# Cross-attention block on one core: score units worked off in sixteen pairs, with the maxima chain, the values' product, the reciprocal chain and the scaling done once for each pair

## The chip, the cores and the metric

The kernel runs on 1 core of one Trainium2 chip. A core has TensorE (PE, matrix products into eight PSUM banks of 128 x 512 fp32), VectorE (DVE), ScalarE (ACT), GpSimd (POOL) and SyncE (SP, which here issues all DMAs). PEld is PE's weight load. The metric is device microseconds of one execution; a kernel's time is the median of its runs. Everything is fp32.

## The reference

x and ctx are 8 sequences of 256 tokens by 512 channels. The block has 16 heads of 32 channels and an MLP of width 2048:

```
q = (layer_norm(x, ln1) @ q_w + q_b) ; k, v = ctx @ k_w + k_b , ctx @ v_w + v_b      # split in 16 heads of 32
scores = einsum("bhqd,bhkd->bhqk", q, k) / sqrt(32) ; scores = where(mask, scores, finfo.min)
out = einsum("bhqk,bhkd->bhqd", softmax(scores), v)
hidden = out @ cproj_w + cproj_b + x
y = gelu_tanh(layer_norm(hidden, ln2) @ fc_w + fc_b) @ proj_w + proj_b
return hidden + y
```

## The kernel before, in words

The eight sequences are worked in two groups g = 0, 1 of four. Every large product (q, k, v, the output projection o, and the MLP's fc and pd) is cut as in Strassen's method into seven products P1 to P7 of quarter matrices, summed up in three PSUM banks X, Y and W; the quarters are first added to one another on DVE or POOL, and the results leave PSUM by additions on DVE and copies on ACT.

Nothing is ordered by the hardware or by a scheduler. The kernel first records all operations (`Order.op`), each with the engines it may run on; `Order.run` then replays them in the order of a long list of words, `PROGRAM`. A word is an operation's name, and ":V", ":A" or ":G" behind it chooses DVE, ACT or POOL. A second list, `PLACES`, says which SBUF slot or PSUM bank each buffer takes. So the order on each engine, and what each buffer waits for, stand in these two tables. In tiles that take the same place one after another, the trace shows one of the names.

The attention has 32 units: a group g, four of the 16 heads (hg) and one sequence b. For each:

- `scores` (L1020 on): eight row-tiled matmuls (32 rows, 256 columns, the group "s" on PE) put k times q, keys in the partitions and queries along the row, into four banks. Eight evictions ev (L614, ACT, 128x256) add the mask's bias and write pr.
- the maxima chain: two transposing reductions of 128x1024 (L1033, DVE), three small copies mc that bring the partitions' quarters together (L1039, ACT), a fold of 32x256 to 32x32 (L1040, DVE), a 32x32 transpose (L1042, DVE), a store md to DRAM, and a load mm that broadcasts the maxima to all partitions (512 KB). Each store and load goes through SP's queue.
- less (L1053 on DVE, as one 128x1024, or L1057 on POOL, as two 128x512) subtracts the maxima, exp (L1060, ACT) takes the exponential, for each of two halves.
- in units of kind "z" ss (L625) adds the two key halves of the weights, so that the sums over keys need four ones-matmuls; in units of kind "p" there is no ss, and eight ones-matmuls. `KINDS` holds the kind of each unit: 16 are "z" and 16 are "p".
- `attend`: the column-tiled group av on PE writes the sums (from the ones-matmuls) and the eight values' products into the two halves of one bank. Then the reciprocal chain on DVE, a reduction (L1083), a reciprocal (L1085) and a transpose (L1086), and the scaling att = av * r (L625, 128x256).

PE works in three tilings: full for the large products, row-tiled for s and column-tiled for av. Units of a group come in an order of their own (`units_of`), and PROGRAM spreads them among the products of k, v, q of group 1, of o and of fc.

Of the kernel before, what the change touches and what calls it, by code (L numbers as in the profile page):

```python
# [21 lines left out]
SLOTS = {"Q": (45, 1024), "P": (36, 512), "H": (14, 256), "sm": (10, 32), "mx": (3, 352)}  # L22

BANKS = ("W", "C")
# [12 lines left out]
class Op:  # L37
    __slots__ = (
        "n", "alts", "fn", "deps", "users", "vt", "bufs", "name", "mode", "table", "serve", "base", "start",
        "end", "eng", "stream", "waiting", "ready", "lead", "psum_of", "after", "lock", "pieces",  # L40
# [3 lines left out]
class Order:  # L44
# [9 lines left out]
    def op(self, name, alts, reads, writes, fn, mode="full", table=None, serve=0.0, base=0.0, lead=0.0, lock=False, pieces=1):  # L54
# [5 lines left out]
        o.deps, o.users, o.vt, o.bufs, o.lead = [], [], None, [], lead  # L60
        o.start = o.end = o.eng = None
# [61 lines left out]
cq0_00_0 turn_c0_10_0 turn_c0_00_0 vw00 c0_10_0:A c0_00_0:V small v0_0_P1a cq0_00_1 turn_c0_00_1 c0_00_1:A cq0_01_1  # L123
turn_c0_10_1 v0_0_P1b c0_10_1:V v0_1_P1a cq0_01_0 turn_c0_11 cq0_11_0 c0_11:V vw10 cq0_11_1 kw00 vw11 v0_0_t1:A
turn_c0_01 cq0_10_0 cq0_10_1 c0_01:V c0t1:V v0_1_P1b v0_1_t1:A rows1 vws1:V turn_c0_31 turn_c0_21 vws3:G c0_21:A rows7
vws2:G c0_31:A k0_1_P1 xt0_3 vw01 k0_0_P1 rows3 turn_c0_20 c0t2:V fw0_11_0 v0_0_P6 stats_x0_11 c0t3:V vws4:V rows0
turn_c0_30 fw0_11_1 fw0i4_1:G v0_0_t2:A xt0_2 aggr_x0_11 rows2 v0_1_P6 stats_x0_10 c0_20:A aggr_x0_10 kw10 v0_0_P5
rows5 c0_30:A eps_x0_1 v0_0_P2 rows4 rows6 fw0_10_0 c0t4:V v0_1_t2:V v0_0_t3:A pow_x0_1 nb_x0_1 norm_x0_11:A mk kw11
rows8 v0_1_P2 fw0_00_1 v0_0_P3 kws3:V mk~1 fw0i4_3:G fw0_10_1 cols fw0_00_0 xt0_5 v0_1_P5 fw0i4_2:V xt0_6 fw0i4_4:V
kws1:V kws2:V cols~1 k0_0_t1:A k0_1_t1:V xt0_0 k0_1_P6 v0_0_c11 xt0_7 fw0_01_0 fw0s3:V v0_1_t3:A xt0_1 fw0s1:G  # L130
fw0i5_1:G v0_1_c11 stats_x0_31 k0_0_P7 stats_x0_21 k0_1_t2:A fw0i5_2:G kw01 xt0_4 fw0_01_1 fcd0_5_False fcd0_7_False
stats_x0_00 fw0i5_3:V fw0i1_1:V fcd0_4_True fw0i7_1:G fw0i1_3:V k0_0_P6 qw00 k0_0_t2:A aggr_x0_00 fw0i7_2:V fw0i7_4:V
v0_1_P3 fw1_01_0 k0_1_P2 k0_0_P5 fw0i1_2:V fw0s2:V norm_x0_10:A aggr_x0_21 fw1_00_0 qw11 aggr_x0_31 fw0i5_4:V qw01
fw0i1_4:V k0_1_P5 vd0_0_11 stats_x0_01 aggr_x0_01 fw1_01_1 eps_x0_0 v0_1_c12:A kws4:G fw0i7_3:V v0_0_c12:A stats_x0_20
# [24 lines left out]
k1_0_t1:A c1t2:G k1_1_P6 exp020_1 ev030_31 ev030_20 ev030_11 k1_0_c11 mc010_1 mc010_2 mc010_3 c1t3:G kd0_1_12
ss020_0:V ev030_10 kd0_1_21 mm022 xt1_4 k1_0_P6 k1_0_t2:A ss020_1:V xt1_0 av020 stats_x1_31 mx030_1 mx030_0 aggr_x1_31  # L160
fold010 k1_1_t2:A s012 xt1_6 stats_x1_30 ev012_21 fcd1_7_True mc030_2 mc030_1 ev012_31 xt1_1 r020 k1_1_P5 stats_x1_01
att020 mf010 k1_0_P5 mm002 mc030_3 aggr_x1_30 xd1_2 kd0_0_22 k1_0_P7 less022_1:G exp022_1 md010 less022_0:G
stats_x1_00 ev012_20 exp022_0 ss022_0:V ev012_01 vd0_0_21 ku011 less002_1:V ev012_00 k1_0_t3:A mm010 less002_0:V
ev012_30 ev012_11 ev012_10 aggr_x1_01 k1_1_t3:A fold030 vd0_0_12 ss022_1:G av022 c1t4:G exp002_0 s032 vu010 xt1_5
vu030 ev032_30 ev032_11 mf030 aggr_x1_00 k1_0_c22 mx012_1 vd0_1_11 k1_1_P3 ev032_10 ev032_20 ss002_0:G mx012_0 k1_0_P3
ku001 ev032_01 ev032_31 eps_x1_3 eps_x1_0 ev032_00 less010_1:V exp002_1 k1_1_P7 ss002_1:G k1_0_P4 ev032_21 mx032_1
exp010_1 k1_0_c12:A mx032_0 vd0_0_22 stats_x1_20 av002 mc032_2 md030 mc032_3 ku021 mc032_1 k1_0_c21 r022 fold032
att022 mf032 k1_1_c12:A ku003 pow_x1_0 r002 mc012_1 s001 stats_x1_21 mc012_3 att002 k1_1_P2 less010_0:G ss010_1:G
exp010_0 vu011 nb_x1_0 mm030 k1_1_c22 ss010_0:G ev001_11 aggr_x1_21 ev001_31 vu012 pow_x1_3 ev001_30 md032 vu032 ku031
ev001_00 ev001_01 ev001_21 aggr_x1_20 av010 ev001_10 ev001_20 s021 ku023 k1_1_c11 k1_1_P4 norm_x1_01:A eps_x1_2  # L170
# [336 lines left out]
def tile_xattn_block(  # L507
# [41 lines left out]
    halves = {}  # L549

    def tile_of(b):
        if b.t is None:
# [917 lines left out]
    with tc.manual_schedule():  # L1470
        for o in order:
            o.fn(o.eng)
# [41 lines left out]
```

## Time and profile before

| | |
|---|---|
| median of 3 runs | 655.94 us (653.59 to 657.04) |
| span of the profiled execution | 652.0 us |
| PE busy | 644.3 us |
| DVE busy | 583.2 us |
| POOL busy | 395.9 us |
| ACT busy | 346.1 us |
| granted PE clock, all stages | 1.00 |

The profile is of one execution, and its span is 3.9 us shorter than the median of the runs, so what is worked out from the profile is compared with 652.0 us first. An engine's busy time is the time that its instructions took, not the time that the kernel would save without them: only an idle gap of PE, or work of PE, is surely in the way. A row of groups reads: line, engine, operation, written tile <- read tiles, shape, count, then busy time in all, mean ns of one, and the idle time ahead of them with what ended it.

### The profile page before, as it was taken

To read this page: it belongs to the slowest core of one execution; us is meant where nothing else is said; L and a number is where in the kernel's file an instruction comes from. 1 tells how busy PE (TensorE), PEld (TensorE's weight loads), DVE (VectorE), ACT (ScalarE), POOL (GpSimd) and SP (SyncE) were. 2 spreads that over 40 slices of the span, in tenths; PEclk is the share of its full clock that TensorE was granted. 3 is DMA by queue.
4 is the path that set the end of the run, shared out by engine and by line. 5 is a ranking of instruction groups with operands and counts; after the bars stand their busy time and mean duration, and the time that the engine had idled before them with its cause. 6 is when DMAs were issued, how large, how long until landed. Compare 5 with 4: busy or idle time off the path is not lost.

```text
span 652.0 us, 11225 instructions
## 1 busy us (share of the span) xinstructions
PE 644.3 (99%) x3793; PEld 487.7 (75%) x3793; DVE 583.2 (89%) x985; ACT 346.1 (53%) x709; POOL 395.9 (61%) x351
## 2 busy tenths in 40 slices
PE   9999999999999999999999999999999999999997
PEld 7755463477545776777787888888888888888886
DVE  4989998999999999999999999988878777999975
ACT  2244698999999879966864645220121222523000
POOL 2543675879987897898859756335813265321244
PEclk9999999999999999999999999999999999999999
DMA  8999998778875447787867787897989989677765
GB/s 268 306 328 324 239 251 284 226 204 152 217 224 151 130 168 232 260 267 250 257 214 250 225 272 232 293 314 170 160 222 197 215 198 204 158 190 227 173 138 97
DMA packets 206713, 144.83 MB, mean 222 GB/s; under 512 B 117136, under 2 KB 167104, under 8 KB 206656
## 3 DMA queue, kind: packets, MB, share of 16 engines
q1 hardware_dynamic: 206656, 144.11, 78.0%
q8 instruction: 30, 0.49, 0.3%
q14 instruction: 27, 0.22, 0.1%
HBM read 104.10 MB, written 39.98 MB: 221 GB/s over the span
## 4 chain that ended last, share of the span: by engine, by line
PE 90%; DVE 4%; ACT 2%; issue 1%; DMA 1%; POOL 1%; DVEq 0%
PE pd_X L634 15%; PE fc_X L634 15%; PE fc_W L634 7%; PE pd_W L634 7%; PE av L634 6%; PE q_X L634 4%; PE v_X L634 4%; PE fc_Y L634 4%; PE k_X L634 4%; PE pd_Y L634 4%; PE s L634 4%; PE o_X L634 2%; PE v_W L634 2%; PE k_W L634 2%; PE o_W L634 2%; DVE mx L1033 2%
## 5 line engine op out<-in xcount | busy, mean ns | idle before, releaser
L614 ACT ACTIVATE pr<-s,cols 128x256 f32<-128x256 f32 x256 | 102.9, 485 | 10.7 <-PE s L634 8.2
L1057 POOL TENSOR_TENSOR pr<-pr,mm 128x512 f32<-128x512 f32 x70 | 90.2, 1318 | 7.2 <-DMA xt<-in_x_dram 5.0
L1237 ACT ACTIVATE h<-h,cols 128x256 f32<-128x256 f32 x128 | 55.2, 499 | 61.2 <-DVE h L625 45.2
L1033 DVE TRANSPOSE_TENSOR_REDUCE mx<-pr 128x32 f32<-128x1024 f32 x64 | 76.9, 1216 | 1.5 <-ACT pr L614 1.3
L1060 ACT ACTIVATE pr<-pr 128x1024 f32<-128x1024 f32 x64 | 66.5, 1061 | 12.1 <-POOL pr L1057 9.0
L625 DVE TENSOR_TENSOR h<-fc_X,h 128x512 f32<-128x512 f32 x80 | 52.4, 675 | 5.5 <-PE fc_X L634 4.7
L625 POOL TENSOR_TENSOR ss<-pr 128x512 f32<-128x512 f32 x24 | 31.5, 1325 | 14.2 <-ACT pr L1060 11.8
L625 DVE TENSOR_TENSOR h<-fc_W,h 128x512 f32<-128x512 f32 x48 | 32.0, 677 | 5.0 <-PE fc_W L634 4.4
L1053 DVE TENSOR_TENSOR pr<-pr,mm 128x1024 f32<-128x1024 f32 x29 | 35.2, 1229 | 0.0
L1039 ACT COPY mx<-mx 32x64 f32<-32x64 f32 x96 | 23.2, 243 | 15.9 <-DVE mx L1033 14.7
L623 POOL TENSOR_TENSOR z1t<-h,z1t 128x512 f32<-128x512 f32 x6 | 8.0, 1360 | 26.1 <-PE pd_Y L634 12.3
L625 POOL TENSOR_TENSOR tq<-tq,rq 128x512 f32<-128x512 f32 x8 | 10.1, 1272 | 21.7 <-DMA rq<-hd 15.4
L634 PE MATMUL pd_X<-z0i,pl 128*128 128x256 f32 x96 | 22.5, 379 | 0.0
L634 PE MATMUL fc_W<-y1i,fl 128*128 128x256 f32 x84 | 20.7, 379 | 0.0
L625 DVE TENSOR_TENSOR h<-fc_Y,h 128x512 f32<-128x512 f32 x24 | 15.9, 672 | 5.3 <-PE fc_Y L634 5.3
L634 PE MATMUL pd_W<-z1i,pl 128*128 128x256 f32 x88 | 20.6, 379 | 0.0
L1040 DVE TENSOR_REDUCE mx<-mx 32x32 f32<-32x256 f32 x32 | 18.4, 578 | 2.2 <-ACT mx L1039 2.0
L634 PEld LDWEIGHTS pd_X<-z0i,pl 128*128 128x128 f32 x96 | 18.2, 190 | 2.5
L811 POOL TENSOR_TENSOR rs_y<-rs_y,neg_half 128x2 f32<-128x2 f32 x8 | 10.2, 1289 | 15.3 <-DMA pl<-prd 7.7
L634 PE MATMUL pd_X<-h,pl 128*128 128x256 f32 x80 | 18.9, 379 | 0.0
L601 ACT COPY h<-fc_X 128x512 f32<-128x512 f32 x16 | 9.0, 594 | 18.5 <-PE fc_X L634 15.6
L625 DVE TENSOR_TENSOR po<-pd_X,po 128x256 f32<-128x256 f32 x24 | 9.9, 414 | 9.6 <-PE pd_X L634 9.4
(574 smaller groups left out, 1857.3 us busy)
## 6 DMA issues: line engine op xcount, KB each, us to landing
pl<-prd SPq DMA_DIRECT2D x65, 256.0 KB, 3.7
mm<-md SPq DMA_DIRECT2D x32, 512.0 KB, 4.3
fl<-fcd SPq DMA_DIRECT2D x40, 256.0 KB, 4.5
fw<-in_L_xattn_fc_w_dram SPq DMA_DIRECT2D x16, 256.0 KB, 4.0
hid<-in_x_dram SPq DMA_DIRECT2D x8, 512.0 KB, 5.8
pw<-in_L_xattn_proj_w_dram SPq DMA_DIRECT2D x32, 128.0 KB, 4.1
hd<-hid SPq DMA_DIRECT2D x8, 512.0 KB, 4.9
fcd<-fw0i SPq DMA_DIRECT2D x7, 512.0 KB, 7.1
```

What stands on the lines that cost most here:

```text
L601: (nc.scalar.copy if e == "ACT" else nc.vector.tensor_copy)(to(), of_())
L614: lambda e: nc.scalar.activation(to(), of_(), AF.Identity, bias=bias(), scale=1.0))
L625: E[e].tensor_tensor(to(), in0(), in1(), op)
L634: nc.tensor.matmul(o(), l(), r(), start=first, stop=True, skip_group_check=True)
L811: lambda e, rs=rs: nc.gpsimd.tensor_tensor(tile_of(rs)[:, 2:4], tile_of(rs)[:, 0:2], neg_half[:, 0:2], ALU.pow), lock=True)
L1033: T.op(f"mx{u}_{h}", [("DVE", 1.126)], [(pr[h], None)], [(mx, [h])], lambda e, h=h: nc.vector.tensor_reduce(tile_of(mx)[:, 0:64].rearrange ...
L1039: lambda e, a=a: nc.scalar.copy(tile_of(mx)[0:32, 64 * a : 64 + 64 * a], tile_of(mx)[32 * a : 32 * a + 32, 0:64]))
L1040: T.op(f"fold{u}", [("DVE", 0.38)], [(mx, [0, 1, 2, 3, 4])], [(mx, [5])], lambda e: nc.vector.tensor_reduce(tile_of(mx)[0:32, 256:288], ti ...
L1053: nc.vector.tensor_tensor(p_, p_, m_[:, None, :].to_broadcast([P, 2, 512]), ALU.subtract)
L1057: E[e].tensor_tensor(p_, p_, m_, ALU.subtract)
L1060: lambda e, h=h: nc.scalar.activation(tile_of(pr[h]), tile_of(pr[h]), AF.Exp), table="exp")
L1237: lambda e, f=f, b=b, c=c: nc.scalar.activation(at(h[f][b], c), at(h[f][b], c), AF.Gelu_apprx_tanh, bias=col(c_fcb + f * 4 + c), scale=1.0 ...
```

## The change

Units (b, b+1) of the same four heads form a pair (`pairs_of`). For each pair, not for each unit:

- the maxima of both units go to one mx tile. kmp (DVE, 128x64) takes the larger of the two key halves, three copies mcp (ACT) follow, foldp (two small DVE maxima, 32x128 and 32x64), mfp (DVE transpose of 32x64) and one store mdp. The broadcast loads mm, less and exp stay one for each unit.
- one group avp on PE: the sums of both units go to one bank (avs), the values' products to another (avo).
- one reciprocal chain rp on 128x512 and one multiplication attp of 128x512.

The scores of a unit go to two tiles of two neighbouring banks each (a new kind of bank tile, "D"), and four evictions ew of 128x512, each with a stride across the two banks, take the place of eight. The other banks become halves of such pair tiles, and a new function `by_bank` states their dependences bank by bank. `KINDS` is now by pairs, and 2 of the 16 pairs are "z" (4 units); the rest have eight ones-matmuls a unit and no ss. The second group of warm-up matmuls has a bank of its own and stands ahead of the first transposes, the bias addition xb on POOL comes in two halves, and PROGRAM and PLACES are written anew. The core of the diff:

```diff
-SLOTS = {"Q": (45, 1024), "P": (36, 512), "H": (14, 256), "sm": (10, 32), "mx": (3, 352)}
+SLOTS = {"Q": (46, 1024), "P": (36, 512), "H": (14, 256), "sm": (14, 32), "mx": (3, 384)}
-BANKS = ("W", "C")
+BANKS = ("W", "C", "D")
...
-KINDS = ("zzzzzzzzzzpppppp", "ppppppppppzzzzzz")
+KINDS = ("pppzzppp", "pppppppp")
...
-        sb = [Buf(f"s{u}_{j}", "C", 2) for j in range(4)]
+        sb = [Buf(f"s{u}_{h}", "D", 2) for h in range(2)]
...
-            for j in range(4):
-                copy(f"ev{u}_{j}{kc}", (pr[j // 2], [2 * kc + j % 2]), (sb[j], [kc]), ..., 256, ...)
+            for h in range(2):
+                copy(f"ew{u}_{h}{kc}", (pr[h], [2 * kc, 2 * kc + 1]), (sb[h], [kc]), ..., 512, ...)
...
+        T.op(f"kmp{u}", [("DVE", 0.16)], [(mx, [0, 1, 2, 3])], [(mx, [4])], lambda e: nc.vector.tensor_tensor(
+            tile_of(mx)[:, 128:192], tile_of(mx)[:, 0:64], tile_of(mx)[:, 64:128], ALU.max))
...
+        def fold(e):
+            t = tile_of(mx)
+            nc.vector.tensor_tensor(t[0:32, 0:128], t[0:32, 128:256], t[0:32, 256:384], ALU.max)
+            nc.vector.tensor_tensor(t[0:32, 128:192], t[0:32, 0:64], t[0:32, 64:128], ALU.max)
...
-        av = Buf(f"av{u}", "C")
+        avs, avo = Buf(f"avs{u}", "C"), Buf(f"avo{u}", "C")
...
-            t = tile_of(rc)[:, 0:8]
+            t = tile_of(rc)[:, 0:16]
...
+    def pairs_of(g):
+        return [((g, hg, b), (g, hg, b + 1)) for hgs in ((0, 2), (1, 3)) for b in (0, 2) for hg in hgs]
...
+        for n, pair in enumerate(pairs_of(g)):
+            mx = Buf(f"mx{g}{pair[0][1]}{pair[0][2]}", "mx", 10)
+            made = [scores(*pair[k], mx, k) for k in range(2)]
+            md = maxima(g, pair, mx)
+            sums_of = [softmax(made[k][0], made[k][2], md, k, KINDS[g][n] == "z") for k in range(2)]
+            attend(g, pair, made, sums_of)
```

What the new order looks like on two engines. On PE before, around the values' product of unit 030 (g, hg, b) while group 1's v is made; s003 is the scores group of another unit, av030 the bank that it writes, ss030 the halves' sum, pr the weights, vu the values:

```order
L634 MATMUL s003_2_1459<-xt0_5_395,ku003_1285 128x256
L634 MATMUL s003_3_1461<-xt0_5_395,ku003_1285 128x256
L634 MATMUL av030_1492<-ss030_1467,ones_89 32x256 x4
L634 MATMUL av030_1492<-pr030_0_1030,vu030_1208 32x256 x2
L634 MATMUL av030_1492<-pr030_1_1028,vu030_1208 32x256 x2
```

And the product of the pair of units 030 and 031 after, which now stands among the products of group 1's q (the sums' and the values' banks show under one name, avs030):

```order
L614 MATMUL avs030_1735<-pr030_0_1356,ones_89 32x256 x2
L614 MATMUL avs030_1735<-pr030_1_1354,ones_89 32x256 x2
L614 MATMUL avs030_1735<-pr031_0_1398,ones_89 32x256 x2
L614 MATMUL avs030_1735<-pr031_1_1394,ones_89 32x256 x2
...
L614 MATMUL avs030_1735<-pr030_0_1356,vu030_1414 32x256 x2
L614 MATMUL avs030_1735<-pr030_1_1354,vu030_1414 32x256 x2
```

Four ones-matmuls on ss030 are gone, and sixteen stand there for the two units, ahead of sixteen products of the values in the same group. On PE as a whole there are 48 column-tiled matmuls more, and changes between the three tilings fall from 89 to 81.

On DVE before, the maxima chain of the first unit, 000, amid the sums of the MLP's weights (fw) and the combining of q (xt0):

```order
L1033 TENSOR_REDUCE mx000_744<-pr000_0_717 128x2x16
L802 BN_STATS st_x1_1_699<-v0_0_21_333 128x6
L1033 TENSOR_REDUCE mx000_744<-pr000_1_715 128x2x16
L625 TENSOR_TENSOR xt0_3_297<-q0_0_W_664,xt0_3_297 128x512
L625 TENSOR_TENSOR fw1i5_752<-fw1s1_672 128x256
L625 TENSOR_TENSOR fw1i7_755<-fw1s3_686 128x256
L804 BN_AGGR mv_x1_1_732<-st_x1_1_699 128x2
L1040 TENSOR_REDUCE mx000_744<-mx000_744 32x32
L625 TENSOR_TENSOR xt0_5_395<-q0_1_Y_712,xt0_5_395 128x512
L625 TENSOR_TENSOR fw1i4_696<-fw1i4_696,fw1_11_573 128x256
L1042 STREAM_TRANSPOSE mx000_744<-mx000_744 32x32
```

And after, the chain of the first pair, units 000 and 001:

```order
L1009 TENSOR_REDUCE mx000_688<-pr000_0_670 128x2x16
L605 TENSOR_TENSOR xt0_7_358<-k0_0_X_264,xt0_7_358 128x512
L1009 TENSOR_REDUCE mx000_688<-pr000_1_667 128x2x16
L788 TENSOR_SCALAR rs_x1_1_715<-mv_x1_1_641 128x2
L1009 TENSOR_REDUCE mx000_688<-pr001_1_712 128x2x16
L1009 TENSOR_REDUCE mx000_688<-pr001_0_718 128x2x16
L1018 TENSOR_TENSOR mx000_688<-mx000_688 128x64
L725 STREAM_TRANSPOSE c1_00_746<-cb1_0_585 128x512
L1026 TENSOR_TENSOR mx000_688<-mx000_688 32x128
L1027 TENSOR_TENSOR mx000_688<-mx000_688 32x64
L1029 STREAM_TRANSPOSE mx000_688<-mx000_688 32x64
```

Four reductions now stand ahead of one chain of small operations, and that chain waits for the second unit's scores as well.

More of the change, by code (lines that the diff above doesn't have):

```diff
@@ L39 @@
         "n", "alts", "fn", "deps", "users", "vt", "bufs", "name", "mode", "table", "serve", "base", "start",
-        "end", "eng", "stream", "waiting", "ready", "lead", "psum_of", "after", "lock", "pieces",
+        "end", "eng", "stream", "waiting", "ready", "lead", "psum_of", "after", "lock", "pieces", "touched",
     )
@@ L547, in tile_xattn_block @@
     E = {"PE": nc.tensor, "DVE": nc.vector, "ACT": nc.scalar, "POOL": nc.gpsimd, "SP": nc.sync}
-    halves = {}
+    halves, pairs = {}, {}
     def tile_of(b):
@@ L562, in tile_of @@
                 b.t = slots.tile([P, SLOTS[b.kind][1]], F32, tag=f"{b.kind}{b.slot}", name=b.name)
-            else:
-                b.t = banks.tile([P, 512], F32, tag=f"B{b.slot}", name=b.name)
+            elif b.kind == "D":
+                b.t = banks.tile([P, 1024], F32, tag=f"D{b.slot // 2}", name=b.name)
+                pairs[b.slot // 2] = None
+            else:
+                s, k = divmod(b.slot, 2)
+                if pairs.get(s) is None:
+                    pairs[s] = banks.tile([P, 1024], F32, tag=f"D{s}", name=b.name)
+                b.t = pairs[s][:, ts(k, 512)]
         return b.t
@@ L641, in tile_xattn_block, with small @@
     nc.vector.memset(warm, 1.0)
-    first = banks.tile([P, 512], F32, tag="B0", name="first")
-    def small(n):
+    first = banks.tile([P, 1024], F32, tag="D0", name="first")
+    def small(n, t):
         for _ in range(n):
-            nc.tensor.matmul(first[:64, :64], warm, warm, start=True, stop=True, skip_group_check=True)
-    small(WARM)
+            nc.tensor.matmul(t[:64, :64], warm, warm, start=True, stop=True, skip_group_check=True)
+    small(WARM, first)
     neg_half = const.tile([P, 4], F32, name="neg_half")
@@ L1064, in scores @@
                      lambda two=two: two()[:, 0], lambda two=two: two()[:, 1], 512, pool_too=True)
[L1065 to L1078 removed]
+        return ss
@@ L1088, in attend @@
-        scale(g, hg, b, u, av, R)
+            t = tile_of(rc)[:, 0:16]
+            nc.vector.tensor_reduce(t, tile_of(avs).rearrange("p (n r) -> p n r", r=32), axis=mybir.AxisListType.X, op=ALU.max, apply_transpose=True)
+            nc.vector.reciprocal(tile_of(rc)[:, 16:32], t)
+            nc.vector.transpose(tile_of(R).rearrange("p (n r) -> p n r", r=32), tile_of(rc)[:, 16:32, None].to_broadcast([P, 16, 32]))
+        T.op(f"rp{u}", [("DVE", 1.68)], [(avs, None)], [(R, None), (rc, None)], inverse)
@@ L1090, in mlp_weight_sums @@
+        A = att[g][hg // 2][b // 2]
+        key = 2 * (hg % 2)
+        plus(f"attp{u}", (A, [key, key + 1]), (avo, None), (R, None), lambda: at(A, key, 2), lambda: tile_of(avo), lambda: tile_of(R), 512, op=ALU.mult)
     def mlp_weight_sums(name, s, load_quarter, put, tiles):
@@ L1373, in attention_inputs @@
         if g == 0:
-            T.op("small", [("PE", 0.1)], [], [], lambda e: small(WARM2))
+            ps = Buf("ps_small", "C")
+            T.op("small", [("PE", 0.1)], [], [(ps, None)], lambda e: small(WARM2, tile_of(ps)))
         if g == 0:
@@ L1401, in attention, with biased @@
         T.stream(f"core{g}")
-        units = units_of(g)
-        made = {}
-        for n in range(len(units) + LOOK):
-            if n < len(units):
-                made[n] = scores(*units[n], KINDS[g][n] == "z")
-            if n >= LOOK:
-                attend(*units[n - LOOK], *made.pop(n - LOOK))
+        for n, pair in enumerate(pairs_of(g)):
[4 more added lines that the diff above has]
+            attend(g, pair, made, sums_of)
+    def biased(e, h):
+        if e == "DVE":
+            v = tile_of(h).rearrange("p (i n) -> p i n", i=2)
+            nc.vector.tensor_tensor(v, v, cb.t[:, None, :].to_broadcast([P, 2, D]), ALU.add)
+            return
+        for i in range(2):
+            nc.gpsimd.tensor_tensor(at(h, i, 1, 512), at(h, i, 1, 512), cb.t, ALU.add)
     def output(g, W):
@@ L1427, in output @@
             T.op(f"xb{g}_{b}", [("POOL", 2.315), ("DVE", 1.14)], [(h, None), (cb, None)], [(h, None)],
-                 lambda e, v=v: E[e].tensor_tensor(v(), v(), cb.t[:, None, :].to_broadcast([P, 2, D]), ALU.add), lock=True)
+                 lambda e, h=h: biased(e, h), lock=True, pieces=2)
         for tp in range(2):
@@ L1467, in tile_xattn_block, with place, meet, by_bank @@
     proj(1, h1)
+    def place(b):
+        return {("Q", b.slot // 2, h) for h in (0, 1)} if b.kind == "Q" else {("Q", b.slot // 2, b.slot % 2)} if b.kind == "P" else {(b.kind, b.slot)}
+    def meet(o, d):
+        if d in o.deps:
+            return True
+        return any(a is not b and place(a) & place(b) for a in o.bufs for b in d.bufs
+                   if a.kind in SLOTS and b.kind in SLOTS)
+    KNOWN = mybir.DependencyInfo(mybir.DependencyClass.Sync, mybir.DependencyReason.DATA)
+    past = {}
+    def by_bank(o, made):
+        for b in {b for b, _ in o.touched if b.kind in BANKS and b.kind != "D"}:
+            tile_of(b)
+            pair, k = pairs[b.slot // 2], b.slot % 2
+            name = pair.tensor.name
+            mine = [i for i in made if any(
+                getattr(x, "bass_ap", None) is not None and x.bass_ap.tensor.name == name and x.bass_ap.offset % 1024 // 512 == k
+                for x in list(i.ins) + list(i.outs))]
+            writes = (b, True) in o.touched
+            written, read = past.setdefault((name, k), ([], []))
+            others = [(d, j) for d, j in past.get((name, 1 - k, "all"), []) if d.eng != o.eng]
+            kept = [j for d, j in others if meet(o, d)]
+            for i in mine:
+                for d, j in written + read:
+                    if d.eng != o.eng:
+                        tc.add_manual_dep(i, j.name, KNOWN, reason="same bank")
+                for d, j in others:
+                    if d in o.deps:
+                        tc.add_manual_dep(i, j.name, KNOWN, reason="operands")
+                for e in ENGINES:
+                    if e != o.eng:
+                        tc.declare_no_dep(i, group=f"{name}_{1 - k}{e}", keep=kept, reason="the pair's other bank")
+            for i in mine:
+                tc.add_to_no_dep_group(f"{name}_{k}{o.eng}", i)
+                past.setdefault((name, k, "all"), []).append((o, i))
+            last = [(o, i) for i in mine[-(4 if o.mode in ("row", "col") else 1):]]
+            if writes:
+                past[name, k] = (last, [])
+            else:
+                read.extend((o, i) for i in mine)
     order = T.run()
@@ L1471, in tile_xattn_block @@
         for o in order:
+            n = len(nc.cur_bb.bb.instructions)
             o.fn(o.eng)
+            if any(b.kind in BANKS for b in o.bufs):
+                by_bank(o, list(nc.cur_bb.bb.instructions)[n:])
 _L = "L0_xattn_"
```

727 lines of the change are left out of this document (351 added, 376 removed).

## The prediction

> **What bounds the kernel now.** I read the page's totals first, then the busy time by stage, then what TensorE (PE) waited for, then its timeline. From the page:
>
> ```profile
> span 652.0 us, 11225 instructions
> PE 644.3 (99%) x3793; PEld 487.7 (75%) x3793; DVE 583.2 (89%) x985; ACT 346.1 (53%) x709; POOL 395.9 (61%) x351
> PEclk9999999999999999999999999999999999999999
> PE 90%; DVE 4%; ACT 2%; issue 1%; DMA 1%; POOL 1%; DVEq 0%
> ```
>
> PE is busy 99% of the span, at full clock throughout, and makes up 90% of the chain that ended last. By stages (columns: stretch, its length, busy time of PE, PEld, DVE, ACT, POOL with instruction counts, PE clock, DMA share, GB/s):
>
> ```profile
> 0.00:60.00 60.00, 59.02 (x246) 39.13 (x247) 46.96 (x83) 21.58 (x33) 26.97 (x35) 1.00 0.94 309
> 60.00:120.00 60.00, 58.50 (x319) 29.48 (x318) 56.59 (x97) 46.60 (x106) 36.69 (x33) 1.00 0.92 264
> 120.00:180.00 60.00, 59.82 (x472) 38.43 (x471) 55.72 (x103) 58.17 (x125) 52.70 (x43) 1.00 0.76 189
> 180.00:250.00 70.00, 68.69 (x580) 43.35 (x582) 69.13 (x120) 63.82 (x136) 60.11 (x44) 1.00 0.54 171
> 250.00:320.00 70.00, 69.73 (x600) 52.62 (x592) 68.23 (x128) 56.38 (x108) 59.68 (x58) 1.00 0.80 257
> 320.00:372.00 52.00, 52.00 (x290) 43.08 (x283) 50.60 (x83) 31.56 (x58) 39.15 (x40) 1.00 0.73 230
> 372.00:470.00 98.00, 98.00 (x473) 85.34 (x472) 88.88 (x141) 30.61 (x65) 54.14 (x43) 1.00 0.84 241
> ```
>
> Attention lies between 60 and 372 us. From 60 to 320 VectorE (DVE) is busy 249.7 of 260 us, nearly as full as PE (256.7). Yet PE loses only 3.3 us there, and nothing from 320 to 470. So DVE's fullness costs PE little; it is cover that is nearly used up, not the bound. What PE waited for by name:
>
> ```profile
> PE k_W L634 <- DVE mx L1042: 1.5, 1, 1.5
> PE o_W L634 <- ACT pr L614: 1.0, 1, 1.0
> PE first L646 <- DVE warm L641: 1.0, 1, 1.0
> PE av L634 <- ACT pr L614: 0.3, 1, 0.3
> ```
>
> That is 3.8 us, 1.0 of it before anything that the change touches. To it comes a scores group that stretched (timeline of PE; start, duration):
>
> ```profile
> 103.21 0.64 PE L634 MATMUL av<-ss,ones 128*32 128x256 f32 x8
> 103.66 1.05 PE L634 MATMUL av<-pr,v 128*32 128x256 f32 x16
> 104.64 1.15 PE L634 MATMUL s<-q,qw 32*128 32x256 f32 x16
> 105.71 3.70 PE L634 MATMUL k_X<-c1t,kws 128*128 128x512 f32 x8
> 214.34 1.90 PE L634 MATMUL s<-v,k 32*128 32x256 f32 x16
> 216.16 1.99 PE L634 MATMUL o_X<-ows,a0t 128*128 128x256 f32 x8
> ```
>
> A scores group occupies PE for 1.07 us (104.64 to 105.71), the one at 214.34 for 1.82: 0.75 us of waiting inside the group. Each matmul shows as two records. So what the change can relieve on PE is 2.8 + 0.75, say 3.5 us, and all else of the span is PE at work. **A gain larger than that must come from less PE work, and the change gives PE more.**
>
> **The change part by part.**
>
> *Sums of the weights.* Of 32 units 16 now add their two halves first (ss) and take four ones-matmuls; after, 4 do (two pairs), and 28 take eight. The groups of all instructions of each kind:
>
> ```profile
> L634 PE MATMUL av<-pr,ones 128*32 128x256 f32 x256 | 17.1, 382 | 0.0
> L634 PE MATMUL av<-ss,ones 128*32 128x256 f32 x128 | 10.2, 390 | 0.4 <-ACT pr L614 0.3
> ```
>
> Sixteen units each: 17.1/16 = 1.07 us against 10.2/16 = 0.64, so 0.43 us more for each of 12 units: **+5.2 us**. The timeline agrees: the eight records from 103.21 to 103.66 are 0.45 us for four matmuls. PE is full around them, so all of it is on the path. In return 24 ss adds go, 18 of them from POOL.
>
> *Values' product in one group for a pair.* The number of score and value matmuls stays. The group changes the array's tiling; the same rows show what that costs: eight records in 0.45 us make 0.90 for sixteen, and the sixteen from 103.66 took 0.98 to the next start, which is row-tiled: 0.08 us. Elsewhere I take 0.1. In the order of PE, changes between full, row-tiled and column-tiled work fall from 89 to 81: **-0.7 us**. The Trainium skill, "TensorEngine Tiling (Array Packing)", Key Properties, says that changing the mode drains the engine; the trace agrees that a change is not free, at 0.08 us here.
>
> *Evictions, maxima, reciprocals, scaling.* None of these is PE's work. The rows:
>
> ```profile
> L614 ACT ACTIVATE pr<-s,cols 128x256 f32<-128x256 f32 x256 | 102.9, 485 | 10.7 <-PE s L634 8.2 <-issue 1.2 <-ACT xn_y L822 0.6
> L614 ACT ACTIVATE att<-att,cols 128x512 f32<-128x512 f32 x16 | 11.3, 719 | 1.0 <-DVE att L625 0.9
> L1039 ACT COPY mx<-mx 32x64 f32<-32x64 f32 x96 | 23.2, 243 | 15.9 <-DVE mx L1033 14.7
> L1040 DVE TENSOR_REDUCE mx<-mx 32x32 f32<-32x256 f32 x32 | 18.4, 578 | 2.2 <-ACT mx L1039 2.0
> L1042 DVE STREAM_TRANSPOSE mx<-mx 32x32 f32<-32x32 f32 x32 | 5.7, 183 | 0.2
> L1083 DVE TRANSPOSE_TENSOR_REDUCE rc<-av 128x8 f32<-128x256 f32 x32 | 13.5, 420 | 0.2
> L1085 DVE RECIPROCAL rc<-rc 128x8 f32<-128x8 f32 x32 | 6.5, 203 | 1.1
> L1086 DVE STREAM_TRANSPOSE r<-rc 128x256 f32<-128x256 f32 x32 | 14.3, 446 | 1.2
> L625 DVE TENSOR_TENSOR att<-av,r 128x256 f32<-128x256 f32 x32 | 12.5, 401 | 0.2
> L625 DVE TENSOR_TENSOR ss<-pr 128x512 f32<-128x512 f32 x8 | 5.3, 678 | 0.8 <-POOL ss L625 0.6 <-ACT pr L1060 0.2
> ```
>
> ACT: 128 evictions of 128x512 at 719 ns, 92.0 us, in place of 102.9; 48 copies fewer, -11.6: about -22 us. The new ones read PSUM with a stride over two banks, which no row shows; between 719 ns and two old ones (970) the total moves from -22 to +10 us, and since ACT is busy only 53% I take the first. DVE: the chain now costs 18.4+5.7+13.5+6.5+14.3+12.5 = 70.9 us. Anew, for each of 16 pairs: three small maxima and one small transpose at about the 183 ns of the small transpose (0.73); the reduction, reciprocal, transpose and product on twice the width, bounded by one and two of the old (1.47 and 2.94 us); nearest to double, say 2.4. That is 16 x 3.1 = 50 us: **about -21 us of DVE**, and six of its eight ss (-4 us) go as well. All of this lies beside PE, so it is worth only the 3.5 us above. Its hidden price is latency: the maxima chain now starts when the second unit of a pair is done, and one store feeds both broadcast loads. In the order the PE work that lies between a unit's load and the product that needs it does not fall below that of before, so I cost it at nothing; without that cover a wait would be about the one of 1.5 us above.
>
> *Banks in pairs.* A scores group now needs two whole pairs of adjacent banks, where four single ones of any place did. That is a new wait with no row of its own. Below: nothing, as the 31 other groups now. Above: the 0.75 us of the group at 214.34, times 32 = 24 us. I take the lower end for the forecast, since ACT empties a group in four instructions, not eight, and has some 22 us less to do; the upper end makes a rival.
>
> *Order.* Warm-up matmuls move ahead of the first transposes: nothing to +0.5 us at the start. The tail issues the same operations: 0 to 1 us, with more stores ahead of the last on SP's queue. POOL gets some 40 more instructions, mostly pieces of 128x512, in the MLP stage, where PE had no wait and POOL was busy 54.14 of 98 us: nothing.
>
> **Sum.** 652.0 + 5.2 - 0.7 = 656.5 us with the waits as they are. With DVE some 25 us and ACT some 22 us lighter, most of the 3.5 us should go; I take 2.9: **span 653.6**. The median of the runs shown (655.94) lies 3.9 us above the profiled span, so **657.5 us**, +0.2%. About 0.5% (3.3 us) is what a measurement of this kernel can tell from no change: 652.7 to 659.2.
>
> **Rivals.**
>
> *Bank pairs bind (slower).* PE stops at the start of scores groups until ACT has emptied the last of four particular banks. For it: 32 groups, one of which already stretched by 0.75 us. Against it: ACT's load falls. From a mean of 0.05 us a group on top of the forecast (1.6 us) it crosses to slower; at 0.2 us it is +6.4: span 660.0, median 663.9. The Trainium skill, "TensorEngine Tiling (Array Packing)", Gotcha 1, names this: row tiles must write different PSUM banks, so row tiling raises the pressure on PSUM. The stretched group bears it out once in 32.
>
> *DVE and POOL collide (slower).* A pair that overlapped, and what the same shapes take elsewhere:
>
> ```profile
> 226.93 3.56 POOL L1057 TENSOR_TENSOR pr<-pr,mm 128x512 f32<-128x512 f32 x2 [1.05 <-DMA mm<-md]
> 227.12 2.24 DVE L625 TENSOR_TENSOR a0t<-att,a0t 128x1024 f32<-128x1024 f32 x1
> L1057 POOL TENSOR_TENSOR pr<-pr,mm 128x512 f32<-128x512 f32 x70 | 90.2, 1318 | 7.2 <-DMA xt<-in_x_dram 5.0
> L625 DVE TENSOR_TENSOR a1t<-att,a1t x2: 1210/1218/1227, 377.8 to 387.2; 128x1024 f32<-128x1024 f32 x2
> ```
>
> POOL's two took 1.78 us each in place of 1.32, DVE's 2.24 in place of 1.22: +1.0 us. The change puts more on POOL; if four such delays reach PE, that is +4.1: span 657.7, median 661.6. Against it: at 227 us PE ran on. The Trainium skill, "SBUF — State Buffer", Who interferes with whom, makes it an exclusive lock between GpSimd and a DVE instruction with two SBUF inputs; these rows agree.
>
> *The relief doesn't come (slower).* The waits move but sum to as much: 656.5, median 660.4.
>
> *All waits go.* 656.5 - 3.5 = 653.0, median 656.9, still no change.
>
> *Faster.* It would take a span under 648.8, 4.2 us below even that; only if the extra sums filled gaps that the rows don't show. The scatter of the runs (lowest 653.59) leaves a little room.
>
> **How the numbers follow.** Forecast 0.36, all waits gone 0.20: no change 0.56. Bank pairs 0.22, relief missing 0.09, collisions 0.07: slower 0.38. Faster 0.06. The range: below, all waits gone (656.9) less the 2.4 us by which the lowest run lay under the median and 2 us of unknown gaps, 652.5; above, the bank-pair case at 0.3 us a group, 653.6 + 9.6 + 3.9 = 667.
>
> **What would show it.** Right: the ones-matmuls' groups about 5 us larger; PE's busy time near 649; its named waits under 1.5 us in attention; scores groups at 1.07 us; DVE's busy time from 60 to 320 us well under 249. Wrong: scores groups longer than 1.2 us, or a wait of PE on ACT's evictions in many places (bank pairs); DVE or POOL means above those quoted (collisions); or a span under 650, which would mean that the eight-matmul sums cost PE less than the rows say.

## The result, and the profile after

The kernel after takes 679.8 us (median of 4 runs, 675.0 to 680.6), against 654.9 us beside it: a ratio of 1.037 (95% interval 1.0325 to 1.0406). It is slower by 25 us, beyond the top of the range. The span of its profiled execution is 678.8 us, 26.8 more than before's 652.0.

The page's totals and its chain of waits, after:

```profile
span 678.8 us, 11129 instructions
PE 656.1 (97%) x3889; PEld 494.5 (73%) x3889; DVE 594.3 (88%) x892; ACT 306.1 (45%) x522; POOL 453.4 (67%) x391
PE 68%; DVE 22%; DMA 4%; issue 3%; POOL 2%; SPq 1%; ACT 1%; DVEq 0%; POOLq 0%; ACTq 0%
```

ACT is lighter by 40 us, more than the 22 of the forecast. DVE is not lighter, though some 25 us had been forecast: it does 93 instructions fewer and is busy 11 us longer. DVE's share of the chain that ended last went from 4% to 22%. The stages (stretch, length, busy time of PE, PEld, DVE, ACT, POOL, PE clock, DMA share, GB/s):

```profile
60.00:120.00 60.00, 59.23 (x314) 29.73 (x313) 56.64 (x77) 36.76 (x60) 39.78 (x41) 1.00 0.87 263
120.00:180.00 60.00, 57.82 (x489) 37.45 (x487) 56.89 (x90) 43.74 (x71) 43.65 (x36) 1.00 0.72 181
180.00:250.00 70.00, 63.62 (x472) 38.18 (x464) 68.35 (x83) 50.11 (x81) 59.35 (x44) 1.00 0.48 152
250.00:320.00 70.00, 64.75 (x585) 47.88 (x586) 66.52 (x110) 44.01 (x67) 53.09 (x50) 0.95 0.73 236
```

PE now loses 14.6 us from 60 to 320 (3.3 before), and most of it from 180 on, where DVE is fullest. The granted clock sinks to 0.95 in the last stretch: another 70 x 0.05 = 3.5 us. What PE waited for, longest first:

```profile
PE k_W L614 <- DVE hid L605: 2.6, 3, 1.3
PE avs L702 <- ACT xn_y L802: 2.3, 1, 2.3
PE s L614 <- DVE h L605: 2.3, 1, 2.3
PE fc_Y L614 <- DMA pl<-prd: 1.8, 1, 1.8
PE o_W L614 <- DVE hid L605: 1.5, 2, 1.3
PE s L614 <- DVE q L605: 1.2, 1, 1.2
PE s L614 <- DVE att L605: 1.1, 1, 1.1
PE k_W L614 <- DVE vw L605: 1.1, 1, 1.1
```

Six of these eight rows, 9.8 of the 13.9 us, wait for DVE, at many places and each for another result; of the other two one ends with ACT and one with a DMA. It is not one new wait: DVE as a whole is late. The rows that say why are those of the new maxima chain (line, shape, count, busy time, mean ns):

```profile
L1027 DVE TENSOR_TENSOR mx<-mx 32x64 f32<-32x64 f32 x16 | 15.9, 996 | 0.5
L1018 DVE TENSOR_TENSOR mx<-mx 128x64 f32<-128x64 f32 x16 | 10.0, 625 | 0.4
L1026 DVE TENSOR_TENSOR mx<-mx 32x128 f32<-32x128 f32 x16 | 9.1, 566 | 2.1 <-ACT mx L1022 2.1
L1029 DVE STREAM_TRANSPOSE mx<-mx 32x64 f32<-32x64 f32 x16 | 3.6, 227 | 0.3
L1027 DVE TENSOR_TENSOR mx<-mx x16: 211/1178/1254, 79.6 to 368.7; 32x64 f32<-32x64 f32 x16
```

The smallest of the three maxima takes 211 ns at best and 1178 in the median (the three numbers are least, median and most). The 48 maxima together take 35.0 us; sixteen times the shortest of each line (0.224, 0.262 and 0.211) would be some 11. What they wait for is seen on the timeline of DVE and POOL side by side:

```profile
190.25 0.47 DVE L1026 TENSOR_TENSOR mx<-mx 32x128 f32<-32x128 f32 x1 [0.82 <-ACT mx L1022]
190.54 2.57 POOL L1416 TENSOR_TENSOR hid<-hid,cb 128x512 f32<-128x512 f32 x2
190.75 1.19 DVE L1027 TENSOR_TENSOR mx<-mx 32x64 f32<-32x64 f32 x1
...
229.86 0.27 DVE L1026 TENSOR_TENSOR mx<-mx 32x128 f32<-32x128 f32 x1
229.88 3.73 POOL L1048 TENSOR_TENSOR pr<-pr,mm 128x512 f32<-128x512 f32 x2
230.16 1.18 DVE L1027 TENSOR_TENSOR mx<-mx 32x64 f32<-32x64 f32 x1
231.27 1.21 DVE L1044 TENSOR_TENSOR pr<-pr,mm 128x1024 f32<-128x1024 f32 x1
```

POOL starts two additions of 1.28 us each in the mean at 190.54, while L1026 is still there; L1027 is called at 190.75 and ends at 191.94, just after POOL's first addition (190.54 + 1.28 = 191.82). At 230 the picture is the same. Nothing of it shows as a wait: the profile gives L1027 no idle time with a releaser here, and the time is booked as DVE's busy time.

### The profile page after: what moved, and what is told of

Same layout as the page of the kernel before. It is cut to its first block, busy times and chain, and to the rows that moved or that the text cites. A ratio compares the mean times of both kernels' runs of the same rounds, so it can differ in the third digit from the quotient of the medians.

```text
span 678.8 us, 11129 instructions
## 1 busy us (share of the span) xinstructions
PE 656.1 (97%) x3889; PEld 494.5 (73%) x3889; DVE 594.3 (88%) x892; ACT 306.1 (45%) x522; POOL 453.4 (67%) x391
## 4 chain that ended last, share of the span: by engine, by line
PE 68%; DVE 22%; DMA 4%; issue 3%; POOL 2%; SPq 1%; ACT 1%; DVEq 0%; POOLq 0%; ACTq 0%
PE fc_Y L614 22%; PE fc_X L614 13%; PE fc_W L614 11%; DVE mx L1009 5%; PE k_X L614 4%; PE ps_c L614 4%; PE k_W L614 3%; DVE pr L1044 3%; DVE mx L1027 2%; PE s L614 2%; PE v_X L614 2%; PE ps_small L614 2%; PE avs L614 1%; DVE hid L605 1%; PE avo L614 1%
## 5 line engine op out<-in xcount | busy, mean ns | idle before, releaser
L1048 POOL TENSOR_TENSOR pr<-pr,mm 128x512 f32<-128x512 f32 x72 | 98.6, 1396 | 28.0 <-DMA mm<-md 21.5
L594 ACT ACTIVATE pr<-s,cols 128x512 f32<-128x512 f32 x128 | 80.0, 687 | 26.3 <-PE s L614 21.0
L605 DVE TENSOR_TENSOR h<-fc_Y,h 128x512 f32<-128x512 f32 x71 | 47.4, 680 | 7.4 <-PE fc_Y L614 7.1
L605 DVE TENSOR_TENSOR h<-fc_X,h 128x512 f32<-128x512 f32 x34 | 23.0, 681 | 2.3 <-PE fc_X L614 2.0
L1022 ACT COPY mx<-mx 32x64 f32<-32x64 f32 x48 | 11.6, 243 | 29.1 <-DVE mx L1018 19.9
L614 PE MATMUL fc_Y<-z0i,pl 128*128 128x256 f32 x96 | 22.3, 380 | 1.8 <-DMA pl<-prd 1.8
L614 PEld LDWEIGHTS fc_Y<-z0i,pl 128*128 128x128 f32 x96 | 18.2, 190 | 4.6 <-DVE y L742 2.2
L605 DVE TENSOR_TENSOR h<-fc_W,h 128x512 f32<-128x512 f32 x26 | 17.6, 679 | 3.7 <-PE fc_W L614 3.5
L603 POOL TENSOR_TENSOR z0i<-h,z0i 128x512 f32<-128x512 f32 x8 | 14.8, 1875 | 3.4 <-PE fc_W L614 3.4
L614 PE MATMUL fc_Y<-y1i,fl 128*128 128x256 f32 x68 | 16.8, 379 | 0.0
L1027 DVE TENSOR_TENSOR mx<-mx 32x64 f32<-32x64 f32 x16 | 15.9, 996 | 0.5
```

What stands on the lines that cost most here:

```text
L594: lambda e: nc.scalar.activation(to(), of_(), AF.Identity, bias=bias(), scale=1.0))
L603: nc.gpsimd.tensor_tensor(to()[:, ts(k, 512)], in0()[:, ts(k, 512)], in1()[:, ts(k, 512)], op)
L605: E[e].tensor_tensor(to(), in0(), in1(), op)
L614: nc.tensor.matmul(o(), l(), r(), start=first, stop=True, skip_group_check=True)
L1022: lambda e, a=a: nc.scalar.copy(tile_of(mx)[0:32, 128 + 64 * a : 192 + 64 * a], tile_of(mx)[32 * a : 32 * a + 32, 128:192]))
L1027: nc.vector.tensor_tensor(t[0:32, 128:192], t[0:32, 0:64], t[0:32, 64:128], ALU.max)
```

## The experiments

Theory: **collision**. A DVE instruction with two operands in SBUF and a POOL instruction that reads SBUF do not run side by side; the later one stands until the other ends. The fold of before was one reduction with one operand. The change makes it of two-operand maxima, 48 of them, in a stage in which DVE has no time left. Rival: **pairing**. The pair's chain starts only when both units' scores are done, and score groups need whole pairs of banks; the order, not the form of the instructions, costs the time. A third: the **extra sums** on PE. Differences below are of ratios to before, times 655 us.

**The maxima with one operand** (e1), in the same places of the order:

```diff
-        T.op(f"kmp{u}", ..., lambda e: nc.vector.tensor_tensor(
-            tile_of(mx)[:, 128:192], tile_of(mx)[:, 0:64], tile_of(mx)[:, 64:128], ALU.max))
+        T.op(f"kmp{u}", ..., lambda e: nc.vector.tensor_reduce(
+            tile_of(mx)[:, 128:192], tile_of(mx)[:, 0:128].rearrange("p (k c) -> p c k", k=2), axis=mybir.AxisListType.X, op=ALU.max))
...
-            nc.vector.tensor_tensor(t[0:32, 0:128], t[0:32, 128:256], t[0:32, 256:384], ALU.max)
-            nc.vector.tensor_tensor(t[0:32, 128:192], t[0:32, 0:64], t[0:32, 64:128], ALU.max)
+            nc.vector.tensor_reduce(t[0:32, 0:64], t[0:32, 128:384].rearrange("p (m c) -> p c m", c=64), axis=mybir.AxisListType.X, op=ALU.max)
```

> The kernel after, with kmp and foldp made by reductions that read one operand (two instructions a pair in place of three; same values). Collision theory: the small two-input maxima stood waiting for POOL's instruction (35.0 us of DVE in 48 of them, where the shortest of each kind sum to about 0.7 us a pair, 11 us); the reductions take about 0.9 us a pair, 15 us, whatever POOL does, so some 20 us of DVE go from a stage in which DVE is nearly full, and half or more of it comes back: 664 to 671 us. Pairing theory (the pair's chain waits for both units, and bank pairs hold scores up): the chain has the same order and the same waits, so 676 us or more. Extra sums alone: no change from 679.8.

Measured: 660.8 us, ratio 1.008 (1.0044 to 1.0119). That gives back 2.85%, 19 us of the 24, more than the expected 664 to 671 us. The rows of its maxima chain:

```profile
L1026 DVE TENSOR_REDUCE mx<-mx 32x64 f32<-32x256 f32 x16 | 9.3, 581 | 2.1 <-ACT mx L1022 2.1
L1018 DVE TENSOR_REDUCE mx<-mx 128x64 f32<-128x128 f32 x16 | 4.6, 285 | 0.4
```

The first reads 256 columns where the two maxima of the fold read 384 with both operands, the second the same 128 as before. They take 13.9 us in place of 35.0: 21.1 us of DVE less, 19 us of time less. The pairs, banks and order are those of after, so pairing is not what cost the bulk. PE's busy time falls to 650.2 us at full clock in every stage, close to the 649 of the prediction.

**Instructions that nothing waits for** (e2 and e3: e1 with three small instructions behind each pair's transpose, on a constant tile):

```diff
+        def turned(e):
+            nc.vector.transpose(tile_of(mx)[0:32, 192:256], tile_of(mx)[0:32, 0:64])
+            for _ in range(3):
+                nc.vector.tensor_tensor(warm, warm, warm, ALU.max)                              # e2
+                nc.vector.tensor_reduce(warm[:, 48:64], warm[:, 0:48].rearrange("p (c m) -> p c m", m=3), ...)   # e3
```

> As e1_one_input, with three two-input 128x64 maxima of a constant tile added on DVE behind each pair's transpose, where nothing waits for their result. Collision theory: they wait for POOL as the old ones did, 0.5 to 1 us each, so DVE gets 25 to 45 us back, and the time goes back up by 8 to 18 us over e1_one_input although the maxima's own chain is untouched. If what counted was the length of the chain: within 2 us of e1_one_input.

> As e2_off_chain_two_input, but the three added instructions read one operand (a reduction of 48 columns to 16). Collision theory: each takes about 0.2 us whatever POOL does, 10 us of DVE in all: 0 to 5 us over e1_one_input, clearly under e2_off_chain_two_input. If the number of small DVE instructions is what costs: the same as e2_off_chain_two_input.

Measured: e2 698.7 us, ratio 1.066 (1.0602 to 1.0720); e3 663.7 us, ratio 1.0145 (1.0098 to 1.0191). The added groups, of e2 and of e3:

```profile
L1031 DVE TENSOR_TENSOR warm<-warm 128x64 f32<-128x64 f32 x48 | 35.4, 737 | 1.1
```

```profile
L1031 DVE TENSOR_REDUCE warm<-warm 128x16 f32<-128x48 f32 x48 | 8.9, 185 | 1.1
```

Forty-eight small instructions that no one waits for cost 38 us when they read two operands from SBUF, far more than the 8 to 18 expected, and about 4 when they read one (e3's interval overlaps e1's). The chain is untouched: in e1, e2 and e3 the store of the maxima is issued 0.03 us behind the end of each of the 16 transposes. So neither the length of the maxima's chain nor the number of small instructions is the cause. DVE's time is: 35.4 us of it cost 38 us, though some of that is PE's clock, granted at 0.982 to 0.988 in e2's runs and at 1.00 in e1's.

The trace of e2 shows the collision one instruction at a time. Of the 48 maxima, 35 began while a POOL instruction ran, and each of them ended 0.08 to 0.11 us behind the end of that instruction. The other 13 met none and took 0.17 to 0.23 us.

**One operand moved to PSUM** (e7, e8: e1 with three maxima in the pair's reciprocal chain; x is the pair's sums in PSUM, or the constant tile itself):

```diff
             nc.vector.transpose(tile_of(R).rearrange("p (n r) -> p n r", r=32), ...)
+            for _ in range(3):
+                nc.vector.tensor_tensor(warm, warm, x, ALU.max)
```

> e1_one_input with three 128x64 maxima added in each pair's reciprocal chain, with one operand in SBUF and the other in PSUM (the pair's sums); nothing waits for the result. Collision theory, with the collision lying in the second SBUF operand: they do not wait for POOL, about 0.2 us each, 10 us of DVE: 2 to 6 us over e1_one_input (660.8). If any two-operand instruction of DVE collides, or any short one: as e8_off_chain_sbuf_operand.

> As e7_off_chain_psum_operand, in the same place, but with both operands in SBUF. Collision theory: 0.5 to 1 us each, 25 to 45 us of DVE, and 20 to 40 us over e1_one_input. Otherwise the same as e7_off_chain_psum_operand.

Measured: e7 669.2 us, ratio 1.0205 (1.0174 to 1.0236); e8 687.0 us, ratio 1.0466 (1.0427 to 1.0505). The largest groups of e7, and the group of e8:

```profile
L1088 DVE TENSOR_TENSOR warm<-warm,k_W 128x64 f32<-128x64 f32 x18 | 3.7, 208 | 0.4
L1088 DVE TENSOR_TENSOR warm<-warm,avs 128x64 f32<-128x64 f32 x18 | 3.7, 208 | 0.4
```

```profile
L1088 DVE TENSOR_TENSOR warm<-warm 128x64 f32<-128x64 f32 x48 | 31.1, 648 | 1.1
```

The same operation, shape and place: 208 ns with one operand in PSUM, 648 with both in SBUF. In e7's trace 39 of the 48 began while a POOL instruction ran, and they took 0.18 to 0.22 us like the others. It is the second SBUF operand that collides. e8's 25 us lie in its expected range. e7 costs some 8 us (more than the 2 to 6 expected) for 48 x 0.208 = 10 us of DVE: DVE's time is paid there too, collision or not. A small part may be the bank of the sums, which these maxima hold longer: PE waited for one of them, once, for 0.6 us.

**The change's form of the fold, in the kernel before** (e4):

```diff
-        T.op(f"fold{u}", ..., lambda e: nc.vector.tensor_reduce(tile_of(mx)[0:32, 256:288], ...))
+        def fold(e):
+            t = tile_of(mx)
+            nc.vector.tensor_tensor(t[0:32, 0:128], t[0:32, 0:128], t[0:32, 128:256], ALU.max)
+            nc.vector.tensor_tensor(t[0:32, 0:64], t[0:32, 0:64], t[0:32, 64:128], ALU.max)
+            nc.vector.tensor_tensor(t[0:32, 256:288], t[0:32, 0:32], t[0:32, 32:64], ALU.max)
```

> The kernel before, whose fold is one reduction of one operand, with the fold made by three two-input maxima of 32 partitions (128, 64 and 32 columns) as the change does it; same values. Collision theory: 96 such instructions at 0.5 to 1 us in place of 32 at 0.58 give DVE 35 to 70 us more, and with DVE busy 96% from 60 to 320 us the time rises by 10 to 30 us. Pairing theory: no pair is made here, so the fold's form costs at most 2 us.

Measured: 710.5 us, ratio 1.081 (1.0747 to 1.0877), without any pair; the expected 10 to 30 us were too few. The new groups, from a profile of the longest of its four runs (716.5 us):

```profile
L1042 DVE TENSOR_TENSOR mx<-mx 32x128 f32<-32x128 f32 x32 | 27.9, 872 | 1.9 <-ACT mx L1039 1.7
L1043 DVE TENSOR_TENSOR mx<-mx 32x64 f32<-32x64 f32 x32 | 23.6, 737 | 1.1
L1044 DVE TENSOR_TENSOR mx<-mx 32x32 f32<-32x32 f32 x32 | 21.9, 686 | 1.1
```

They sum to 73.4 us in place of the reduction's 18.4: 55 us of DVE, and 53 us of time. The form of the change's fold alone, three maxima for each of 32 units, does twice the harm of the whole change.

**POOL's instructions cut in two** (e11, from the kernel after):

```diff
-                for k in range(2):
-                    p_ = at(pr[h], k, 1, 512)
-                    E[e].tensor_tensor(p_, p_, m_, ALU.subtract)
+                for k in range(4):
+                    p_ = at(pr[h], k, 1, 256)
+                    E[e].tensor_tensor(p_, p_, at(M, 2 * h + k % 2), ALU.subtract)
```

> The kernel after, with POOL's subtractions of the maxima done in pieces of 128x256 (four instructions in place of two); DVE's instructions are those of after. Collision theory: a DVE instruction that meets one waits for the rest of that instruction, so the wait behind these is at most about 0.75 us and not 1.3; the last of the three small maxima falls from 1.0 us mean to 0.6 to 0.8, POOL takes some 10 us more in all, and the time falls from 679.8 by 2 to 10 us. If the wait does not hang on the length of POOL's instruction: no gain, or slower by POOL's added time.

Measured: 674.2 us, ratio 1.029 (1.0232 to 1.0354), some 5 us under after, though the two intervals overlap. POOL's subtractions became slower in sum, the last maximum shorter:

```profile
L1048 POOL TENSOR_TENSOR pr<-pr,mm 128x256 f32<-128x256 f32 x144 | 112.0, 811 | 21.5 <-DMA mm<-md 6.0 <-ACT pr L594 3.9 <-DVE pr L1044 3.1
L1027 DVE TENSOR_TENSOR mx<-mx 32x64 f32<-32x64 f32 x16 | 12.6, 789 | 0.5
```

Its mean fell from 996 ns to 789 and its median from 1178 to 638, while POOL worked 112.0 us on the subtractions against 98.6. The wait goes with the length of POOL's instruction, as it must if DVE stands until that one ends.

**The extra sums** (e6 adds 48 column-tiled matmuls to the kernel before; e5 takes 48 from e1 and so leaves out part of the values' product):

```diff
-            sums_ = [(..., lambda: ones, lambda j=j: at(ss, j), True) for j in range(4)]
+            sums_ = [(..., lambda: ones, lambda j=j: at(ss, j), True) for _ in range(2 if g == 0 or hg == 3 and b == 1 or hg == 3 and b == 3 else 1) for j in range(4)]   # e6
...
-                       ..., kc == 0) for kc in range(2) for j in range(4)]
+                       ..., kc == 0) for kc in range(1 if g == 0 and not ss else 2) for j in range(4)]   # e5
```

> The kernel before with 48 column-tiled matmuls more: in 12 of its 16 units with ss each of the four ones-matmuls is issued twice, the second writing the same sums again. Nothing else moves. By the rows of before: 48 x 0.108 = 5.2 us, so 659.4 us. If TensorE's gaps took them up: under 656 us.

> e1_one_input without 48 column-tiled matmuls, the number that the change adds: in 12 units of group 0 the second key half of the values' product is left out, so its output is not the reference's. If what is left of the loss is TensorE's extra work: 5.2 us under e1_one_input, about 655.6 us, next to the kernel before (654.2). If the rest of the loss is waits: less than 2 us under e1_one_input.

Measured: e6 659.0 us, ratio 1.0046 (1.0030 to 1.0063), so +3.0 us (2.0 to 4.1), a little under the 5.2; the span of its profiled execution is 656.4, 4.4 more than before's. e5 658.5 us, ratio 1.0061 (1.0030 to 1.0092): 1 us under e1, and the intervals overlap. In e5 PE was busy 4.3 us less than in e1 (645.9 against 650.2), and waits took up most of it. So the same extra work costs 2 to 4 us in the kernel before, and in e1 what is left of the loss is only partly that.

**The start** (e9) and **the evictions** (e10), both on e1; e9 puts the second group of warm-up matmuls back behind the first transposes, e10 splits each pair eviction in two:

```diff
-small cq0_00_0 vw00 turn_c0_10_0 c0_10_0:V turn_c0_00_0 c0_00_0:A v0_0_P1a
+cq0_00_0 vw00 turn_c0_10_0 c0_10_0:V turn_c0_00_0 c0_00_0:A small v0_0_P1a
...
-                copy(f"ew{u}_{h}{kc}", (pr[h], [2 * kc, 2 * kc + 1]), ...)
+                def apart(e, h=h, kc=kc):
+                    for j in range(2):
+                        nc.scalar.activation(at(pr[h], 2 * kc + j), at(sb[h], 2 * j + kc), AF.Identity, bias=..., scale=1.0)
...
```

> e1_one_input with the second group of warm-up matmuls put back behind the first two transposes, in a bank of its own (as in the kernel before). In the trace of after, TensorE's idle time in its first 20 us is 2.3 us more than before. If the start order is what costs it: 1.5 to 2.5 us under e1_one_input (660.8). If it is taken up later: no change.

> e1_one_input with each pair eviction of scores split into two of 128x256, as before; banks, order and all else stay. ACT gets 128 instructions of 485 ns for 64 pairs less: from 80 us to between 103 and 124 us for the evictions. If ACT's time is off the path (busy 184 of 260 us from 60 to 320): within 2 us of e1_one_input (660.8). If the bank pairs are held up by ACT: 3 us over or more.

Measured: e9 660.3 us, ratio 1.0068 (1.0042 to 1.0094); e10 661.7 us, ratio 1.0105 (1.0066 to 1.0144). Neither can be told from e1's 1.0081. By the windows PE was idle in the first 20 us for 1.0 us in before, 1.5 in after and 1.1 in e9, so after's loss there is 0.5 us and not the 2.3 of the expectation. PE's work does come later: the matmuls v_X<-vws,c0t begin at 15.76 us in before, 18.19 in after, 18.32 in e1 and 16.47 in e9. Whether e9's 1.85 us reach the end, these runs can't tell. ACT's evictions, whole or split, are off the path within the 2 us that were expected:

```profile
L1007 ACT ACTIVATE pr<-s,cols 128x256 f32<-128x256 f32 x256 | 100.1, 492 | 20.8 <-PE s L614 17.0 <-POOL pw0i L605 2.8 <-DVE att L605 0.4
```

That is e10's row: 100.1 us against 80.1 with the pair evictions, for no difference in time that these runs resolve. No kernel of the eleven beats the one before.

## Why the prediction was wrong

*The step that failed* is the one that priced the maxima: "three small maxima and one small transpose at about the 183 ns of the small transpose (0.73)" a pair. They measured 0.625 + 0.566 + 0.996 + 0.227 = 2.41 us, so 16 x 1.68 = 27 us more DVE than forecast. That is most of the distance between the 25 us less that were forecast for DVE and the 11 us more that were measured. The row taken was the nearest in size and the wrong one in kind: a transpose reads one operand, these read two from SBUF. A row of the right kind was quoted in the prediction, DVE's 128x1024 addition that took 2.24 us beside POOL in place of 1.22.

*The second step that failed* is "all of this lies beside PE, so it is worth only the 3.5 us above". It holds for a gain, since PE can give back no more than its waits. It does not hold for a loss. With DVE at 250 of 260 us, added DVE time is paid for the most part: +9 us cost 4 (e3), +10 cost 8 (e7), +21 cost 19 (e1 to after), +31 cost 25 (e8), +35 cost 38 (e2), +55 cost 53 (e4). Part of the larger costs is PE's clock, which fell with PE's stops: it was granted at 0.982 to 0.988 in the runs of e2 and e4 and at 0.987 to 0.992 in e8's. As an estimate from these figures, some 10 us of 700 in e2 and in e4 and some 7 in e8 are that. The view that called DVE "cover that is nearly used up" had this in it, and the sum did not use it.

*The rival was named and given 0.07.* It counted collisions by POOL's added work and put four of them on the path. What the change moved was DVE's side: 48 new two-operand instructions in place of 32 reductions that did not collide (in before's trace 28 of them began while a POOL instruction ran, and all 32 took 0.54 to 0.64 us). The Trainium skill, "SBUF — State Buffer", Who interferes with whom, says just that: tensor_tensor with both inputs in SBUF contends with GpSimd's reads, tensor_reduce on trn2 never does, and an instruction with at most one SBUF input, outside the two-port modes, does not. The runs agree with all three (648 ns, 185 and 581 ns, 208 ns). The prediction cited the section for the lock and did not hold the new instructions against it.

*Right.* The extra sums cost 3.0 us of time in e6, 4.4 of its profiled span and 4.8 of PE's busy time (649.1 against 644.3), against 5.2. PE's busy time in e1 is 650.2 against 649. ACT's evictions are off the path. The order's other costs are small: e1, the change without its two-operand maxima, is 0.8% over before (0.44 to 1.19%), against the forecast of 0.2%.

*Bank pairs.* The sign that the prediction gave for them, scores groups longer than 1.2 us, came true without them: after has six such groups (1.21 to 2.84 us up to the next matmul), and 4.6 us of named waits at scores groups, all of which end with a DVE instruction. e1 has the same bank pairs, and 31 of its 32 scores groups take 1.07 or 1.08 us and one 1.44. In before four took longer (1.15, 1.20, 1.33 and 1.83), of which the prediction saw only the last. One named wait is left in e1:

```profile
PE s L614 <- DVE h L605: 1.3, 1, 1.3
```

So the stretching came with the two-operand maxima and not with the bank pairs; that the bank pairs cost something of their own wasn't shown.

*Open.* Of e1's 5 us over before, the sums explain 2 to 4 by e6 and about 1 by e5. The rest, 1 to 4 us, was not pinned down: neither the start nor the evictions could be shown to hold it.

## What to carry to other kernels

When a change swaps one instruction for another that does the same on an engine, price it by a row that has the same number of operands in SBUF, not by one of the same size; a short two-operand DVE instruction also costs what is left of POOL's, here up to 1.3 us in the kernel after. Where an engine beside the bound is nearly full, as DVE was here with 250 of 260 us, gains on it are capped by the bound's waits, but losses aren't: here about half to all of the added time was paid. And an engine's busy time that rises while its instructions fall in number says to look at the least, median and most of its small groups.

## What the runs showed of the hardware beyond this

Of the two maxima of a fold, back to back on DVE, the second pays more in the kernel after: 0.996 us against 0.566, and in the timeline above POOL's next instruction has started (190.54) by the time that the second is called (190.75). It is no rule: in e4 the three means are 0.872 (0.707 without one maximum of 5.98 us), 0.737 and 0.686. That a single instruction of both would pay only once wasn't tried.

A DVE instruction can stand through more than one instruction of POOL. In e4 one maximum took 5.98 us:

```profile
409.07 5.98 DVE L1042 TENSOR_TENSOR mx<-mx 32x128 f32<-32x128 f32 x1
409.16 1.26 POOL L625 TENSOR_TENSOR h<-h,k 128x512 f32<-128x512 f32 x1
...
414.19 0.71 POOL L625 TENSOR_TENSOR pw1i<-pw,pw1i 128x256 f32<-128x256 f32 x1
```

Six POOL instructions ran back to back from 409.16 to 414.90, and the maximum ended at 415.05. Why it did not get its turn between them, as L1027 did at 191.94 in the timeline of after, isn't shown.

A stop of PE of some 2 us costs more than itself. In the kernel after, PE stood 2.33 us before 268.1; the windows around it (columns as above, clock before the last two):

```profile
264.00:268.00 4.00, 1.79 (x36) 0.79 (x27) 3.93 (x12) 3.91 (x6) 3.73 (x5) 1.00 1.04 374
268.00:272.00 4.00, 3.87 (x20) 3.61 (x21) 3.90 (x7) 3.34 (x5) 3.73 (x3) 0.66 0.67 203
272.00:276.00 4.00, 4.00 (x30) 2.97 (x32) 4.00 (x7) 3.83 (x7) 3.36 (x5) 0.91 0.94 303
```

The granted clock was 0.66 and 0.91 in the 8 us behind the stop, which costs 4 x 0.34 + 4 x 0.09 = 1.7 us more. The same came behind a stop of 2.3 us before 292.3 in the same run (0.57 from 293 to 297) and behind one of 2.7 us before 487.7 in e9 (0.57 from 488 to 492). In before, where the longest stop inside the attention was 1.5 us, and in e3, with 1.8, the clock stayed at 1.00 there.
